# Layer 1's first keys and values, computed at the end of layer 0's attention

## The chip, the cores and the metric

The kernel runs on one core of a Trainium2 chip as one program. The metric is the device time of that program in microseconds (us). A core has five engines with a queue of instructions each: TensorE (PE in the profile) multiplies matrices from SBUF into PSUM, VectorE (DVE), ScalarE (ACT) and GpSimd (POOL) compute on SBUF and read PSUM, and SyncE (SP) here issues transfers. The engines wait for each other through semaphores. An instruction that waits holds up everything behind it in its own queue.

## The reference

Two layers follow each other on `x`, 16 sequences of 128 tokens with 256 features. Each layer is a cross-attention to a context `ctx` of the same shape, then a mixture of experts, both gated into the residual:

```python
x = x + tanh(g_xattn[0]) * attention0(layernorm(x), ctx, ctx)   # causal, 16 heads of 16
x = x + tanh(g_ffn[0])   * ffn0(layernorm(x))                   # top 2 of 16 experts + a shared expert
x = x + tanh(g_xattn[1]) * attention1(layernorm(x), ctx, ctx)   # rows of queries masked
x = x + tanh(g_ffn[1])   * ffn1(layernorm(x))                   # top 2 of 8 experts
```

Inside an attention, `q = layernorm(x) @ Wq + bq`, `k = ctx @ Wk + bk` and `v = ctx @ Wv + bv`, then softmax of the scaled products over the keys, times `v`, times `Wo`. What matters for this case: **the keys and values of layer 1 depend on the context and weights alone**, not on what layer 0 computes.

## The kernel before, in words

All of `x` stays in SBUF (`x_sb`, 16 batches side by side). Batches are handled in four groups of four. `attention(layer, ...)` returns the pieces of one layer's attention as functions:

- `load_kv(g)` (line 321) issues on SP the load of group g's context, 512 KB, into the tile `slot_cn`. In layer 1 every group uses the same half of this tile, so a load must wait until the products of the group before have read it.
- `keys(g, m)` (line 333) makes one of two halves of the group's keys: two matrix products (tile `psk`, line 337), and a ScalarE copy with bias into `slot_kq`. `vals(g, i)` (line 343) makes the values of two batches: four products (`psv`, line 348) and a ScalarE copy into `slot_v`. Two buffers each of keys, queries and values alternate by the parity of g.
- `constant()` (line 361) makes the product `bo` of the value bias with `Wo`.
- `q_stats`, `q_rows`, `q_turn`, `q_product` normalise a group's rows (GpSimd raises the variances to a power, tile `mvq`, lines 286 and 287; VectorE writes `xn_q`, line 296), transpose them (`nt_q`) and make the queries (`psq`, line 402).
- `run(...)` (line 599) is the loop over 32 units, a unit being half the heads of one batch. For each unit GpSimd spreads the keys (`kd`, line 429), TensorE makes the scores (`pss`, line 456), VectorE their maxima (`mx`, line 462), ScalarE the exponentials (`exps`, line 472), TensorE transposes them two units later (`pt`, line 484; copies `pT` by ScalarE and VectorE, lines 489 and 491) and multiplies with the values three units later (`pso`, line 505).

`run` has an order written out by hand for TensorE, VectorE and ScalarE (`tc.manual_schedule`). In each unit it calls, in order, the lists `first`, the scores, the transposes, the list `then`, the exponentials, the value products, and the lists `last` and `late`. The argument `fill` puts more calls into these lists. For the units after 34 they are appended to `then`. SP's and GpSimd's orders are left to the framework's planner, which places an instruction by when it expects its inputs.

At the end of layer 0's attention the dictionary `fill0` (line 946) puts in the shared expert: `shared_up(tb, c)` (products `pu`, line 921; Silu on ScalarE, line 927; product `hs` on VectorE, line 928) and `shared_down(tb, i)` (products `po`, line 934; added to `x_sb` on VectorE, line 940). In the same units the routing of the last group goes on: its rows (line 296), transposes (`nt_f`, line 308, called by `route_turn`), logits (`pr`, line 581), the long sequence of small VectorE steps in `send0` (lines 713 to 896), and GpSimd's scatters of the rows (line 852).

The tiles `psk`, `psv`, `po`, `pr`, `py`, `psq`, `pso`, `rank` and `bo` all come from one PSUM pool of two banks, `ps_o`. A product waits until the tile before it in its bank has been copied out.

Then come layer 0's routed experts, in 10 iterations of four tiles: SP fetches the rows (`xg`, line 1005, three buffers), TensorE transposes them (`xt`, line 1016), and the two products follow (lines 1038 and 1063). In this loop the results of group 0 are gathered back by GpSimd (`gather0`, tile `slot_y`, line 978) and added to `x_sb` on VectorE (`add0`, line 987), and group 0's queries for layer 1 are made. A branch that joins all engines follows (line 1119), then layer 1's `run`, with the remaining gathers and adds in its units. While it starts, SP loads 1 MB pieces of layer 1's expert weights (line 1344). The kernel ends with layer 1's experts, each of which adds its result to `xacc` by an indirect transfer (line 1479).

Layer 1's first products stand in two places. Group 0's `load_kv`, `keys`, `vals` and `constant` stand after layer 0's attention, before the first `xt`. Group 1's load is put into iteration 2 of the expert loop, and its `keys` and `vals` into units 0 to 3 of layer 1's `run`, by these lines:

```python
d = int(layer == 1 and g == 1)
if not d:
    put(first, u, load_kv, g)
for m in range(KD):
    put(then, u - d + 1 + m, keys, g, m)
for i in range(0, GB, 2):
    put(then, u - d + 3 + i // 2, vals, g, i)
```

Of the kernel before, what the change touches and what calls it, by code (L numbers as in the profile page):

```python
# [24 lines left out]
def kernel(ctx: ExitStack, tc: tile.TileContext, a: dict, out: bass.AP):  # L25
# [6 lines left out]
    NB, S, D = a["x"].shape  # L32
    assert S == P
    T = NB * S
    KD = D // P
# [4 lines left out]
    GB = 4  # L40
# [3 lines left out]
    E1, F1 = a["L1_ffn_W1"].shape[0], a["L1_ffn_W1"].shape[2]  # L44
# [70 lines left out]
    def load_attn(layer, eng, pool, at={}):  # L115
        pre = f"L{layer}_xattn_"
        w = {}
        for s in ("k", "q"):
            w["W" + s] = load_w(pre + "W" + s, D, eng, pool, at.get(s))
        for s in ("k", "q"):  # L120
            w["b" + s] = load_cols(pre + "b" + s, [P, KD], eng, pool)
        for s in ("v", "o"):
            w["W" + s] = load_w(pre + "W" + s, D, eng, pool, at.get(s))
        w["bv"] = pool.tile([P, KD], F32, name=f"c_{pre}bv", bufs=1)
        with nc.allow_non_contiguous_dma(reason="a column of 256"):
            eng.dma_start(w["bv"], a[pre + "bv"].rearrange("(k p) -> p k", p=P))
        w["bo"] = load_row(pre + "bo", D, eng, pool)
        return w
# [15 lines left out]
    attn_w = [load_attn(0, nc.scalar, ap0, weights_in("y")), {}]  # L144
# [169 lines left out]
    def attention(layer, E, w, dispatch):  # L314
# [109 lines left out]
        def spread(u):  # L424

            b, m = units[u]
            cols = slice((b % GB) * P, (b % GB + 1) * P)
            kd = ap.tile([P, HQ, P], F32, tag="kd", name=f"kd_{layer}_{u}", bufs=3)
            due["pool"] = nc.gpsimd.tensor_tensor(  # L429
                kd,  # L430
                groups[b // GB]["kT"][:, m, cols].unsqueeze(1).broadcast_to([P, HQ, P]),
                heads.unsqueeze(2).broadcast_to([P, HQ, P]),
                ALU.mult,
            )
            kds[u] = kd
# [158 lines left out]
        def route_send(g):  # L594

            rows, lg = routes.pop(g)
            return dispatch(g, lg, rows)

        def run(pool, along, fill, leave=False):


            nonlocal ap
            ap = pool
            NU = len(units)
            first, then, last, late = {}, {}, {}, {}
            senders = {}

            def piece(g):
                if g not in senders:
                    senders[g] = route_send(g)  # L610
                next(senders[g], None)

            def put(where, u, fn, *args):
                where.setdefault(u, []).append((fn, args))

            if layer == 0:
                for i in range(0, GB, 2):
                    put(then, i // 2, vals, 0, i)
                put(then, 2, constant)
            put(last, 3, add_constant, 0)  # L620
            for g in range(1, NG):
                u = (g - 1) * GB * KD

                d = int(layer == 1 and g == 1)
                if not d:
                    put(first, u, load_kv, g)
                for m in range(KD):
                    put(then, u - d + 1 + m, keys, g, m)
                for i in range(0, GB, 2):
                    put(then, u - d + 3 + i // 2, vals, g, i)  # L630
                for i in range(0, GB, 2):
                    put(last, u + d + i // 2, q_stats, g, i)
                    put(last, u + d + 1 + i // 2, q_rows, g, i)
                    put(then, u + d + 2 + i // 2, q_turn, g, i)
                for m in range(KD):
                    put(then, u + d + 5 + m, q_product, g, m)
                put(last, u + 7, add_constant, g)
            for b in range(NB):
                u = b * KD + KD - 1
                put(last, u + 2, inverse, b)  # L640
                put(then, u + 3, turn_inverse, b)
                put(last, u + 3, scale, b)
                put(then, u + 4, output, b)
                g = b // GB
                if b % 2 and not (leave and b == NB - 1):

                    d = int(b < NB - 1)
                    put(last if d else first, u + 5, route_rows, b - 1)
                    put(then, u + 5 + d, route_turn, b - 1, None)
                    put(late, u + 5 + d, route_product, b - 1)  # L650
                    if b % GB == GB - 1:
                        at = list(range(u + 7, u + 7 + MOST))
                        if g == NG - 2:

                            v = NB * KD + (3 if leave else 4)
                            at[SENDS:] = range(v, v + MOST - SENDS)
                            if leave:
                                at = [NB * KD + 1 + i // 2 for i in range(MOST)]
                        if g == NG - 1:
                            at = [u + 5 + (i + 1) // 3 for i in range(MOST)]  # L660
                        for i in at:
                            put(late, i, piece, g)
                put(first, b * KD, along, b)
            for u, fns in fill.items():
                fns = [(fn, args) for fn, *args in fns]
                if u < NU:
                    late[u] = fns + late.get(u, [])
                elif u < NU + 3:
                    then[u] = fns + then.get(u, [])
                else:  # L670
                    then[u] = then.get(u, []) + fns
            with tc.manual_schedule(engines=ENGINES):
                for u in range(2):

                    with tc.issue_after(due["pool"].ins):
                        spread(u)
                u = 0
                while u < NU or first or then or last or late:
                    for fn, args in first.pop(u, []):
                        fn(*args)  # L680
                    if u < NU:
                        if u + 2 < NU:
                            spread(u + 2)
                        scores(u)
                    if 0 <= u - 2 < NU:
                        turn(u - 2)
                    for fn, args in then.pop(u, []):
                        fn(*args)
                    if u < NU:
                        exps(u)  # L690
                    if 0 <= u - 3 < NU:
                        values(u - 3)
                    for fn, args in last.pop(u, []) + late.pop(u, []):
                        fn(*args)
                    u += 1
# [100 lines left out]
    def send0(g, sc, rows):  # L796
# [98 lines left out]
        nc.vector.tensor_reduce(sm, ex, AX.X, ALU.add)  # L895
        nc.vector.tensor_tensor(gate0[:, g, 1, :], sm, gate0[:, g, 0, :], ALU.mult)

    (load_kv, keys, _, _, q_stats, q_rows, q_turn, q_product, run), _ = attention(
        0, E0, attn_w[0], send0
    )  # L900
    load_kv(0)
# [28 lines left out]
    def shared_down(tb, i):  # L930
# [12 lines left out]
        )  # L943

    up, down = shared_up, shared_down
    fill0 = {
        32: [(up, 0, 0)], 33: [(up, 0, 1)], 34: [(up, 1, 0)], 35: [(down, 0, 0), (up, 1, 1)],
        36: [(down, 0, 2), (up, 2, 0)], 37: [(down, 1, 0), (up, 2, 1)],
        38: [(down, 1, 2), (up, 3, 0)], 39: [(down, 2, 0), (up, 3, 1)], 40: [(down, 2, 2)],
        41: [(down, 3, 0)], 42: [(down, 3, 2)],  # L950
    }
    run(ap0, lambda b: None, fill0)
    at0.close()
# [38 lines left out]
    with tc.tile_pool(name="f0", bufs=2, reuse_waits="tile") as fp:  # L992
# [10 lines left out]
        def fetch0(u):  # L1003
            xg = new0("xg", fp.tile, [P, UN, D], F32, tag="xg0", name=f"xg0_{u}", bufs=3)
            nc.sync.dma_start(
                xg, xs0[u * UN * P : (u + 1) * UN * P, :].rearrange("(j p) d -> p j d", p=P)
            )
            return xg
# [48 lines left out]
        def down0(u, hT):  # L1057
# [16 lines left out]
            )  # L1074

        NU = NH0
        dispatch1 = []
        got = [fetch0(0), fetch0(1)]
        (load_kv, keys, vals, constant, q_stats, q_rows, q_turn, q_product, run), route1 = (
            attention(1, E1, attn_w[1], lambda *z: dispatch1[0](*z))  # L1080
        )
        load_kv(0)
        for m in range(KD):
            keys(0, m)
        for i in range(0, GB, 2):
            vals(0, i)
        constant()


        extra, ahead = {}, {}  # L1090
        last = [-(-(2 * GT * (g + 1) + (E0 - 1) * P) // (UN * P)) for g in range(NG - 1)]
        assert last[0] + 4 == last[1] + 2 == last[2] == NU
        add = lambda where, u, fn, *args: where.setdefault(u, []).append((fn, args))
        u = last[0]
        add(extra, 2, load_kv, 1)
        for t in range(GB):
            add(extra, u, gather0, t)
        for i in range(0, GB, 2):
# [55 lines left out]
    ap1 = ctx.enter_context(tc.tile_pool(name="at1", bufs=2, reuse_waits="tile"))  # L1154
# [368 lines left out]
    def down_n(n):  # L1523
# [2 lines left out]
            out_rows if n >= len(order) - NL else xacc,  # L1526
        )

    run(ap1, beside, {
        **{KD * b + 1 + (b > 0): [(add0, t), (add0, t + 1)] for b, t in comes.items()},  # L1530
        31: [(get, 0), (get, 1)],
        33: [(turn_in, 0), (up_n, 0)],
# [8 lines left out]
    route_rows, route_turn, route_product, route_send = route1  # L1541
# [84 lines left out]
```

## Time and profile before

| | |
|---|---|
| median of 3 runs | 817.59 us (816.72 to 818.86) |
| the profiled execution's own time | 819.49 us |
| its span | 817.8 us |
| TensorE matrix products, busy | 739.6 us (90%) |
| VectorE, busy | 454.8 us (56%) |
| ScalarE, busy | 360.8 us (44%) |
| GpSimd, busy | 302.3 us (37%) |
| last `pu` of the shared expert starts | 238.43 us |
| first `psk` of layer 1 (group 0) starts | 251.43 us |
| first `xt` of the experts of layer 0 starts | 259.18 us |
| first `pss` of layer 1 starts | 337.91 us |

The span runs from the first to the last instruction of the profiled execution; times in the timelines count from its start. In a timeline, a row is a run of equal instructions: start, duration, engine, line, operation, the tile written and the tiles read, how many, and in brackets how long the engine was idle before and which instruction released it. The duration of pipelined matrix products overlaps the next row a little, so starts are better for counting than ends.

### The profile page before, as it was taken

The numbers are of one execution on the slowest core, as the hardware profiler recorded it, in microseconds if no ns is written. First come the engines' busy times: TensorE is split into PE (matmuls) and PEld (weight loads), VectorE is DVE, ScalarE is ACT, GpSimd is POOL, SyncE is SP. The second block draws the span as 40 slices with busy tenths as digits, with TensorE's granted clock in tenths as the row PEclk, the third lists the DMA queues.
The fourth block names the chain that finished last, engine by engine and source line by source line (L and its number), as shares of the span: only waits on it lengthen the run. The fifth ranks groups of instructions, "written<-read, shape, count | busy, mean of one in ns | idle before, by whom it ended". The sixth has DMA issues, their size and how long they took to land.

```text
span 817.8 us, 14876 instructions
## 1 busy us (share of the span) xinstructions
PE 739.6 (90%) x4960; PEld 550.0 (67%) x4960; DVE 454.8 (56%) x1214; ACT 360.8 (44%) x1431; POOL 302.3 (37%) x376
## 2 busy tenths in 40 slices
PE   7999989889898998879988987798999999999993
PEld 3556646555456886445645554687899999999982
DVE  4666698998483334588788779647222222222210
ACT  1677757675032332578767758221112222222220
POOL 6524226341222004763643524256323333223321
PEclk9999999999999999999999979899999999999997
DMA  8999992000015444781210402626766656666633
GB/s 283 377 346 200 343 331 75 14 34 21 26 38 168 138 147 129 257 283 48 70 41 14 156 20 72 239 67 195 241 184 187 196 166 174 190 194 187 178 57 116
DMA packets 88125, 126.80 MB, mean 155 GB/s; under 512 B 8544, under 2 KB 72832, under 8 KB 87888
## 3 DMA queue, kind: packets, MB, share of 16 engines
q1 hardware_dynamic: 75824, 106.41, 40.9%
q0 software_dynamic: 10144, 18.22, 8.8%
q10 hardware_dynamic: 2080, 1.19, 0.5%
q8 instruction: 43, 0.70, 0.4%
q14 instruction: 34, 0.28, 0.1%
HBM read 80.77 MB, written 47.13 MB: 156 GB/s over the span
## 4 chain that ended last, share of the span: by engine, by line
DMA 23%; PE 17%; DVE 10%; issue 3%; ACT 3%; POOL 1%; POOLq 0%; ACTq 0%; DVEq 0%; SPq 0%
DMA xacc<-y,xg 21%; PE pu L1448 4%; PE pss L456 2%; PE po L1469 2%; PE pt L484 2%; DVE mx L462 2%; ACT y L1478 2%; PE pso L505 1%; PE psq L402 1%; PE py L541 1%; DMA out_dram<-xacc 1%; PE psv L348 1%; DVE pT L491 1%; ACT hT L1459 1%; DVE st L283 1%
## 5 line engine op out<-in xcount | busy, mean ns | idle before, releaser
L472 ACT ACTIVATE p<-pss,mx 128x128 f32<-128x128 f32 x512 | 180.8, 390 | 10.2 <-DVE mx L462 10.0
L1448 PE MATMUL pu<-xT,w 128*128 128x128 f32 x1152 | 137.7, 279 | 5.9 <-DVE xT L1438 4.9
L1448 PEld LDWEIGHTS pu<-xT,w 128*128 128x128 f32 x1152 | 136.7, 195 | 9.4 <-DVE xT L1438 6.3
L472 ACT ACTIVATION_READ_ACCUMULATOR p<-pss,mx 128x1 f32 x512 | 117.3, 229 | 0.0
L1479 POOL DMA_INDIRECT xacc<-y,xg x34 | 54.4, 1600 | 146.7 <-ACT y L1478 118.1
L1469 PE MATMUL po<-w_sb,hT 128*128 x432 | 101.1, 384 | 0.6 <-issue 0.3
L429 POOL TENSOR_TENSOR kd<-slot_kq,heads 128x512 f32<-128x512 f32 x64 | 66.7, 1047 | 91.2 <-PE pss L456 88.5
L1478 ACT ACTIVATE y<-yb,gate 128x256 f32<-128x256 f32 x36 | 18.3, 508 | 184.6 <-DMA xacc<-y,xg 161.3
L1461 DVE TENSOR_SCALAR hT<-pu,bT_b 128x128 f32<-128x128 f32 x108 | 30.4, 344 | 123.6 <-ACT hT L1459 123.6
L484 PEld LDWEIGHTS pt<-ident,p 128*128 128x128 f32 x512 | 55.9, 143 | 49.9 <-issue 33.6
L1469 PEld LDWEIGHTS po<-w_sb,hT 128*128 128x128 f32 x432 | 80.4, 193 | 10.8 <-issue 0.6
L462 DVE TENSOR_REDUCE mx<-pss 128x8 f32<-128x1024 f32 x64 | 78.0, 1219 | 16.3 <-PE pss L456 16.2
L456 PE MATMUL pss<-kd,slot_kq 64*128 64x512 f32 x256 | 75.2, 665 | 1.7 <-POOL kd L429 1.2
L484 PE MATMUL pt<-ident,p 128*128 128x128 f32 x512 | 71.7, 283 | 0.9 <-ACT rT L527 0.5
L489 ACT COPY pT<-pt 128x512 f32<-128x512 f32 x64 | 39.4, 616 | 19.4 <-PE pt L484 19.3
L491 DVE COPY pT<-pt 128x512 f32<-128x512 f32 x64 | 43.6, 681 | 0.7 <-PE pt L484 0.7
L505 PE MATMUL pso<-pT,slot_v 128*32 128x128 f32 x1024 | 42.5, 285 | 0.0
L852 POOL DMA_INDIRECT xs<-rows,to x32 | 31.6, 987 | 28.1 <-DVE more L961 13.2
L1038 PE MATMUL pu0p<-w,xT 128*128 x160 | 38.4, 395 | 0.2 <-ACT xT L1021 0.2
L1459 ACT ACTIVATE hT<-pu,bT_b 128x128 f32<-128x128 f32 x108 | 30.8, 368 | 15.7 <-PE pu L1448 15.6
L1476 DVE TENSOR_TENSOR yb<-po,b_sb 128x256 f32<-128x256 f32 x36 | 15.3, 424 | 39.7 <-PE po L1469 39.1
L1225 POOL DMA_INDIRECT xs<-rows,toi x32 | 31.9, 997 | 14.5 <-issue 8.0
(277 smaller groups left out, 1190.3 us busy)
## 6 DMA issues: line engine op xcount, KB each, us to landing
w<-in_L_ffn_W_dram SPq DMA_DIRECT2D x36, 1024.0 KB, 5.2
xs<-zero SPq DMA_DIRECT2D x7, 2080.0 KB, 20.1
w<-in_L_ffn_W_dram SPq DMA_DIRECT2D x12, 512.0 KB, 8.3
xs<-zero SPq DMA_DIRECT2D x1, 6144.0 KB, 22.8
w_sb<-in_L_ffn_W_dram SPq DMA_DIRECT2D x6, 1024.0 KB, 12.9
xg<-xs SPq DMA_DIRECT2D x10, 512.0 KB, 3.8
yb<-y SPq DMA_DIRECT2D x10, 512.0 KB, 3.0
xg<-xs SPq DMA_DIRECT2D x39, 130.0 KB, 2.9
```

The source lines that it names most:

```text
L429: due["pool"] = nc.gpsimd.tensor_tensor(kd, groups[b // GB]["kT"][:, m, cols].unsqueeze(1).broadcast_to([P, HQ, P]), heads.unsqueeze(2).br ...
L456: nc.tensor.matmul(ps[:, j, :], qT[rows, m, cols], kd[rows].rearrange("p h k -> p (h k)"), start=(layer != 0), stop=True,)
L462: nc.vector.tensor_reduce(mx, s, AX.X, ALU.max, negate=True)
L472: nc.scalar.activation(p[:, h, :], s[:, h, :], AF.Exp, bias=mx[:, h : h + 1], accum_out=sums[b][:, m * HH + h : m * HH + h + 1],)
L484: nc.tensor.transpose(pt[:, i * P : (i + 1) * P], p[:, j * HQ + i, :], ident)
L489: nc.scalar.copy(pT, pt)
L491: nc.vector.tensor_copy(pT, pt)
L505: nc.tensor.matmul(o[r * VW : (r + 1) * VW, :], v[:, b % GB, m * HH + h, :], pT[h // HQ][:, (h % HQ) * P : (h % HQ + 1) * P], start=(x == ...
L1448: nc.tensor.matmul(ps[:, j, c * P : (c + 1) * P], wt[:, k, (j * 4 + c) * P : (j * 4 + c + 1) * P], xT[:, k * P : (k + 1) * P], start=(k == ...
L1459: nc.scalar.activation(dst, src, AF.Relu, bias=bias)
L1469: nc.tensor.matmul(po[:, :D], hT[:, c, :], w2_sb[c][:, bass.ds(e256, D)], start=(c == 0), stop=(c == FC1 - 1),)
L1479: nc.gpsimd.indirect_dma_start(out=dst, out_offset=bass.IndirectOffsetOnAxis(ap=xg[:, D : D + 1].bitcast(I32), axis=0), in_=y, in_offset=N ...
```

## The change

Layer 1's `attention(1, ...)` is set up before layer 0's `run` is called, and a function `kv(i)` is added to `fill0`. In the fill of layer 0's last units it issues group 0's load (unit 38), its keys (units 39 and 40, after the shared expert's products of that unit), its values (units 41 and 42, before them), and in unit 43 the whole of group 1: load, keys and values. The calls that did this later are taken out: group 0's before the first `xt`, group 1's load in the expert loop, and group 1's keys and values in layer 1's units 0 to 3. `constant()` stays where it was.

One more step is moved. The transposes of the last two batches' rows for the routing (`route_turn` of batch 14) leave the head of the list `then` of unit 36 and become `turn_last`, called after the first shared product of that unit.

```diff
-                for m in range(KD):
-                    put(then, u - d + 1 + m, keys, g, m)
-                for i in range(0, GB, 2):
-                    put(then, u - d + 3 + i // 2, vals, g, i)
+                for m in range(0 if d else KD):
+                    put(then, u + 1 + m, keys, g, m)
+                for i in range(0, 0 if d else GB, 2):
+                    put(then, u + 3 + i // 2, vals, g, i)
...
-                    put(then, u + 5 + d, route_turn, b - 1, None)
+                    if d:
+                        put(then, u + 6, route_turn, b - 1, None)
...
+    def kv(i):
+
+        if i == 0:
+            load_kv(0)
+        elif i < 3:
+            keys(0, i - 1)
+        elif i < 5:
+            vals(0, 2 * (i - 3))
+        else:
+            load_kv(1)
+            for m in range(KD):
+                keys(1, m)
+            for j in range(0, GB, 2):
+                vals(1, j)
+
+    def turn_last():
+        route0[1](NB - 2, None)
...
-        36: [(down, 0, 2), (up, 2, 0)], 37: [(down, 1, 0), (up, 2, 1)],
-        38: [(down, 1, 2), (up, 3, 0)], 39: [(down, 2, 0), (up, 3, 1)], 40: [(down, 2, 2)],
-        41: [(down, 3, 0)], 42: [(down, 3, 2)],
+        36: [(down, 0, 2), (turn_last,), (up, 2, 0)], 37: [(down, 1, 0), (up, 2, 1)],
+        38: [(down, 1, 2), (up, 3, 0), (kv, 0)], 39: [(down, 2, 0), (up, 3, 1), (kv, 1)],
+        40: [(down, 2, 2), (kv, 2)], 41: [(kv, 3), (down, 3, 0)], 42: [(kv, 4), (down, 3, 2)], 43: [(kv, 5)],
...
-        load_kv(0)
-        for m in range(KD):
-            keys(0, m)
-        for i in range(0, GB, 2):
-            vals(0, i)
         constant()
...
-        add(extra, 2, load_kv, 1)
...
-    run(ap1, beside, {
+    run1(ap1, beside, {
```

More of the change, by code (lines that the diff above doesn't have):

```diff
@@ L896, in send0 @@
         nc.vector.tensor_tensor(gate0[:, g, 1, :], sm, gate0[:, g, 0, :], ALU.mult)
-    (load_kv, keys, _, _, q_stats, q_rows, q_turn, q_product, run), _ = attention(
+    (load_kv, keys, _, _, q_stats, q_rows, q_turn, q_product, run), route0 = attention(
         0, E0, attn_w[0], send0
@@ L945 @@
     up, down = shared_up, shared_down
+    dispatch1 = []
+    (load_kv, keys, vals, constant, q_stats, q_rows, q_turn, q_product, run1), route1 = attention(
+        1, E1, attn_w[1], lambda *z: dispatch1[0](*z)
+    )
+    def kv(i):
[13 more added lines that the diff above has]
+        route0[1](NB - 2, None)
     fill0 = {
         32: [(up, 0, 0)], 33: [(up, 0, 1)], 34: [(up, 1, 0)], 35: [(down, 0, 0), (up, 1, 1)],
-        36: [(down, 0, 2), (up, 2, 0)], 37: [(down, 1, 0), (up, 2, 1)],
-        38: [(down, 1, 2), (up, 3, 0)], 39: [(down, 2, 0), (up, 3, 1)], 40: [(down, 2, 2)],
-        41: [(down, 3, 0)], 42: [(down, 3, 2)],
+        36: [(down, 0, 2), (turn_last,), (up, 2, 0)], 37: [(down, 1, 0), (up, 2, 1)],
+        38: [(down, 1, 2), (up, 3, 0), (kv, 0)], 39: [(down, 2, 0), (up, 3, 1), (kv, 1)],
+        40: [(down, 2, 2), (kv, 2)], 41: [(kv, 3), (down, 3, 0)], 42: [(kv, 4), (down, 3, 2)], 43: [(kv, 5)],
     }
@@ L1076 @@
         NU = NH0
-        dispatch1 = []
         got = [fetch0(0), fetch0(1)]
-        (load_kv, keys, vals, constant, q_stats, q_rows, q_turn, q_product, run), route1 = (
-            attention(1, E1, attn_w[1], lambda *z: dispatch1[0](*z))
-        )
-        load_kv(0)
-        for m in range(KD):
-            keys(0, m)
-        for i in range(0, GB, 2):
-            vals(0, i)
         constant()
```

## The prediction

> **What bounds the kernel now.** I read the page's chain first, then the chain in order of time, then each engine's timeline in two stretches: the end of layer 0's attention (216 to 260 us) and the first units of layer 1's attention (337 to 362 us). Those are the only places that the change touches.
>
> ```profile
> DMA xacc<-y,xg 21%; PE pu L1448 4%; PE pss L456 2%; PE po L1469 2%; PE pt L484 2%; DVE mx L462 2%; ACT y L1478 2%; PE pso L505 1%; PE psq L402 1%; PE py L541 1%; DMA out_dram<-xacc 1%; PE psv L348 1%; DVE pT L491 1%; ACT hT L1459 1%; DVE st L283 1%
> ```
>
> No single engine carries the end. From 580 us on it is one scatter-add after another, and before that it is the attention. All of it runs at fixed distances from what came before, so a microsecond gained or lost at 260 us arrives at the end unless something in between waits for something else. The timeline of TensorE (start, duration, work, idle before it and its releaser) at the end of layer 0's attention:
>
> ```profile
> 212.72 3.60 PE L921 MATMUL pu<-xnT,w_L_ffn_Ws 128*128 128x512 f32 x8
> 219.29 0.76 PE L308 MATMUL nt_f<-ident,rows 128*128 128x128 f32 x4 [2.97 <-DVE rows L296]
> 219.88 1.89 PE L934 MATMUL po<-w_L_ffn_Ws,hs 128*128 128x256 f32 x8
> 221.61 3.60 PE L921 MATMUL pu<-xnT,w_L_ffn_Ws 128*128 128x512 f32 x8
> ...
> 241.87 1.89 PE L934 MATMUL po<-w_L_ffn_Ws,hs 128*128 128x256 f32 x8
> 245.43 2.16 PE L934 MATMUL po<-w_L_ffn_Ws,hs 128*128 128x256 f32 x8 [1.67 <-DVE x_sb L940]
> 249.60 1.99 PE L934 MATMUL po<-w_L_ffn_Ws,hs 128*128 128x256 f32 x8 [2.02 <-DVE x_sb L940]
> 251.43 3.60 PE L337 MATMUL psk<-slot_cn,slot_w 128*128 128x512 f32 x8
> 254.87 3.62 PE L348 MATMUL psv<-slot_w,slot_cn 128*128 128x256 f32 x16
> 258.32 1.03 PE L368 MATMUL bo<-slot_w,c_L_xattn_bv 128*128 128x256 f32 x4
> 259.18 1.04 PE L1016 MATMUL xt<-ident,xg 128*128 128x128 f32 x8
> ```
>
> Here TensorE has three holes, all behind VectorE. Its last work before the experts (group 0's psk, psv, bo) is back to back, and xt, the experts' first transpose, follows with no hole. From there the expert loop is TensorE's: 39.13 us busy between 260 and 300 us. So **the start of xt is the number to work out**. The start-to-start distances are 1.72 for one of the two psk or psv halves (3.44 for a pair), 0.86 for bo, 1.73 for a po.
>
> Then the first units of layer 1, where group 1's products stand now (TensorE, then VectorE):
>
> ```profile
> 340.88 1.13 PE L456 MATMUL pss<-kd,slot_kq 64*128 64x512 f32 x4
> 341.94 1.99 PE L337 MATMUL psk<-slot_cn,slot_w 128*128 128x512 f32 x4
> 345.14 1.13 PE L456 MATMUL pss<-kd,slot_kq 64*128 64x512 f32 x4 [1.21 <-POOL kd L429]
> ...
> 361.45 0.69 PE L523 MATMUL rt<-ident,rs 128*128 128x128 f32 x2 [2.30 <-DVE pT L491]
> ```
> ```profile
> 348.78 0.49 DVE L987 SCALAR_TENSOR_TENSOR x_sb<-slot_y,gate,x_sb 128x256 f32<-128x256 f32 x1 [0.51 <-DMA slot_y<-yb,to]
> 349.18 1.22 DVE L462 TENSOR_REDUCE mx<-pss 128x8 f32<-128x1024 f32 x1
> ...
> 355.63 1.46 DVE L296 TENSOR_SCALAR xn_q<-x_sb,mvq 128x256 f32<-128x256 f32 x2 [1.19 <-POOL mvq L287]
> ```
>
> TensorE is *not* the bound here. It waits for GpSimd's kd, for the pT copies, and 2.30 us before rt. VectorE waits for the gathered rows (slot_y), runs on to 354.4, then waits for GpSimd's mvq. GpSimd is the slow one: eight gathers at about 1.27 us each.
>
> **Part 1, turn_last.** The transpose of the rows of batches 14 and 15 (nt_f) moves from before shared-expert product po(0,2) to after it. nt_f needs VectorE's rows (released at 219.29) and po does not. So po runs at 216.16 to 217.88, inside the old hole; nt_f still starts at 219.29 and the next pu at 219.88 instead of 221.61: **-1.73**. VectorE's following chain starts from ScalarE's Silu of that pu (VectorE idles 3.31 before 225.88), so it moves too: every time below is 1.73 earlier than its old counterpart.
>
> **Part 2, group 0's products between the shared expert's.** In the built kernel's order they stand as pu(3,1), psk, po(2,2), psk, psv, po(3,0), psv, po(3,2). They add no work, but they share two PSUM banks with the po tiles, so each start also waits for an eviction. pu(3,1) ends at 241.87 - 1.73 = 240.14.
> - psk: 240.14 to 241.86. ScalarE evicts it behind the last Silu (old 243.40, now 241.67 to 242.27), 0.69 long: 242.96.
> - po(2,2) takes that bank: 243.05 to 244.77, a hole of 1.19.
> - second psk: its bank is free at 245.37 - 1.73 = 243.64; runs 244.77 to 246.49. Eviction 1.92 after its start (251.43 to 253.35 in the trace), 0.69 long: 247.38. ScalarE's exponential zex before it, which waits for VectorE, ends at 245.85 and does not hold it.
> - psv: same bank, 247.45 to 249.17, a hole of 0.96. po(3,0): 249.17 to 250.89 (VectorE's eviction of po(2,2) ends at 249.5 - 1.73 = 247.8). Second psv 250.89 to 252.61, po(3,2) 252.61 to 254.33.
>
> **Part 3, group 1's load and products before xt.** Group 1's context overwrites the tile (slot_cn) that group 0's last psv reads, so SP's load waits for 252.61 plus about 0.2. Queued behind it on SP are the first three fetches of expert rows (xg), free from 253.67 - 1.73 = 251.95; they start about 1.3 later, land by 257 (median 3.8), and xt needs the first only at 263.9, so this is hidden with 6.9 to spare. Landing of the load, from the tile's view:
>
> ```profile
> DMA to landing us min/median/max: 3.3/7.1/15.0
> ```
>
> I take the low end, 3.3: it is the row of the load at 258.51, in a stretch where the DMA engines are 12 to 42% busy; 7.1 and more belong to stretches that are full. So psk of group 1 starts at 252.8 + 3.3 = 256.15, a hole of 1.8; two psk and two psv end at 256.15 + 4 x 1.72 = 263.03 (evictions on two banks keep up), bo 0.86, **xt at 263.89 against 259.18: +4.7**. Counted another way: +6.9 of products, and the holes, measured start to start, go from about 7.4 to 5.4. With the load at 7.1 it is +8.5; with the three new holes (3.97) gone it is +0.7.
>
> A second SP effect: group 2's load is also hoisted, to behind the third xg fetch (its tile is free when group 1's psv ends). The fetch behind it waits for the first xt anyway: 0.
>
> **Part 4, what layer 1's start gives back.** Removed there: 4 x 1.72 = 6.9 of TensorE, two 0.7 and two 0.6 evictions of ScalarE. The full 6.9 would come back only if TensorE were the bound. Following the waits without these products: the second pss could start at 338.97, so mx(1) comes 0.4 earlier; but the next adds wait for gathers issued at 339.28 to 344.0, after the branch that joins the engines, and the last lands at 348.78. mx(2) stays at 349.18, exps(2) at 350.44, mx(3) at 352.64, then the mvq wait. Give-back: **0** (ends 0 and -2, the latter if the gathers land faster; nearer 0 since no gather moves).
>
> GpSimd's order changes by one step: a kd (1.03) now goes ahead of the mvq pair that VectorE waits for at 355.63. mvq is 1.03 later, but the xn_q that took 1.05 beside the old kd (its twin took 0.40) then runs alone: **+0.2** (ends 0 and +1).
>
> *A rule against the change.* The removal leaves TensorE idle from 340.03 to 345.14. The windows view (start:end, length, busy PE, PEld, DVE, ACT, POOL, granted clock, DMA share, GB/s) after the existing 2.30 us hole:
>
> ```profile
> 359.00:362.00 3.00, 0.70 (x4) 0.29 (x2) 2.39 (x3) 0.59 (x1) 1.56 (x2) 0.87 1.09 369
> 362.00:365.00 3.00, 3.00 (x22) 1.20 (x22) 1.68 (x4) 2.83 (x16) 0.62 (x1) 0.56 0.28 102
> ```
>
> The clock falls to 0.56 and the pso and pss there take 1.08 and 1.90 instead of 0.65 and 1.13: 1.2 lost. The Trainium skill, "TensorE: Matmul & The Clock Gate", Part 1, halves the clock only after an idle window of about 3.4 us; by it, the 2.3 hole should have been harmless and the new one of 5.1 is not. By either the next pss and pt run cold and lose about 1.7 together. I count 0: pss would end at 347.0 and pt at 348.9, and mx(2) starts at 349.18 and the copies of pt after it. With that cover gone the sum is +1.2 more, as in the row. The holes before xt are no longer than the old ones of 2.97 and 2.02, after which the clock stayed at 1.00 in the windows from 195 to 260 us.
>
> **Sum.** -1.73 and the rest of the stretch make +4.7, layer 1 gives 0, GpSimd +0.2: **+4.9**. The profiled execution took 819.49 (span 817.80, 1.69 around it); its sum is span 822.7. It stands 1.9 above the median of the runs shown, 817.59, so the median predicted is 817.6 + 4.9 = **822.5**.
>
> **Rivals.**
> - *Layer 1 gives the products back (not slower).* If TensorE sets units 0 to 3, 6.9 returns: 817.6 + 4.9 - 6.9 = 815.6. For it: pss at 340.88 stands right behind psk, and TensorE is 90% busy over the span. Against it: the 1.21 and 2.30 us waits and the slot_y wait above. It decides once the give-back passes 4.9 - 2.5 = 2.4.
> - *The new holes do not form.* The load or the evictions come sooner and xt is +0.7: 818.5. Against: the load's tile is read until 252.6, and no landing of it is below 3.3.
> - *The load is slow, or the new idle leaves TensorE cold on the path.* +3.8 or +1.2: 823.7 to 826.3. For: 7.1 median. Against: a mostly idle DMA.
> - *turn_last does not do what it says* (VectorE does not follow): +1.73, 824.2.
>
> **How the numbers follow.** Main case (two to three holes, no give-back, 821 to 824): 0.66; slower cases 0.16; holes partly absent or a give-back of some 2 (818.5 to 820.5) 0.10; full give-back 0.08. A measurement of this kernel tells about 0.3% (2.5 us) from no change: 815.1 and 820.0 are the limits. Slower 0.83, same 0.12, faster 0.05. Range 819.0 to 825.2: it leaves out the full give-back and the slow load.
>
> **What would show it.** Right: a hole-free po(0,2) before nt_f; xt 4 to 5.5 us later than 259.2; psk of group 1 released by the DMA of slot_cn, its start about 3.5 after the end of group 0's last psv; rt of unit 4 still waiting for pT, its distance from the first pss of layer 1 (337.91 to 361.45, 23.5) unchanged within 1. Wrong: that distance shorter by 2.5 or more; xt within 2 of 259; or the distance from xt to the end changed elsewhere.

## The result, and the profile after

The changed kernel is slower: 825.66 us median against 818.62 us for the kernel before in the same comparison, **ratio 1.0085, 95% interval 1.0063 to 1.0106** (10 runs each). That is about +7.0 us, where +4.9 was forecast, and the median lies 0.5 us above the stated range. Of the distance to the forecast 822.5, 1.0 us is not the change's: the range was built on three runs of the kernel before (817.59), and in these ten it is 818.62. The profiled execution has a span of 827.6 us; it was the slowest of the ten, so its distances are used below more than its span.

TensorE's timeline at the end of layer 0's attention, kernel after (start, duration, work, idle before it and its releaser):

```profile
212.65 3.60 PE L922 MATMUL pu<-xnT,w_L_ffn_Ws 128*128 128x512 f32 x8
216.08 1.89 PE L935 MATMUL po<-w_L_ffn_Ws,hs 128*128 128x256 f32 x8
219.21 0.76 PE L308 MATMUL nt_f<-ident,rows 128*128 128x128 f32 x4 [1.24 <-DVE rows L296]
219.81 3.60 PE L922 MATMUL pu<-xnT,w_L_ffn_Ws 128*128 128x512 f32 x8
...
236.63 3.60 PE L922 MATMUL pu<-xnT,w_L_ffn_Ws 128*128 128x512 f32 x8
240.07 1.88 PE L337 MATMUL psk<-slot_cn,slot_w 128*128 128x512 f32 x4
242.84 1.99 PE L935 MATMUL po<-w_L_ffn_Ws,hs 128*128 128x256 f32 x8 [0.89 <-ACT slot_kq L341]
244.67 1.88 PE L337 MATMUL psk<-slot_cn,slot_w 128*128 128x512 f32 x4
247.32 1.99 PE L348 MATMUL psv<-slot_w,slot_cn 128*128 128x256 f32 x8 [0.78 <-issue]
249.16 1.89 PE L935 MATMUL po<-w_L_ffn_Ws,hs 128*128 128x256 f32 x8
250.88 1.89 PE L348 MATMUL psv<-slot_w,slot_cn 128*128 128x256 f32 x8
252.61 1.99 PE L935 MATMUL po<-w_L_ffn_Ws,hs 128*128 128x256 f32 x8
257.59 5.37 PE L337 MATMUL psk<-slot_cn,slot_w 128*128 128x512 f32 x8 [2.98 <-DMA slot_cn<-in_ctxT_dram]
262.79 3.62 PE L348 MATMUL psv<-slot_w,slot_cn 128*128 128x256 f32 x16
266.25 1.03 PE L368 MATMUL bo<-slot_w,c_L_xattn_bv 128*128 128x256 f32 x4
267.11 1.04 PE L1041 MATMUL xt<-ident,xg 128*128 128x128 f32 x8
```

Up to 252.61 every start is within 0.25 us of the forecast. Then group 1's psk waits 2.98 us for its load, and the psk pair takes 5.20 from start to start instead of 3.44. xt starts at 267.11 instead of the forecast 263.89 (259.18 before). The same hole and what follows it in the windows view (start:end, length, busy PE, PEld, DVE, ACT, POOL, granted clock, DMA share, GB/s):

```profile
254.00:257.60 3.60, 0.62 (x4) 0.23 (x2) 0.75 (x1) 0.00 (x0) 0.00 (x0) 1.00 0.86 242
257.60:261.20 3.60, 3.60 (x6) 1.65 (x7) 0.00 (x0) 0.69 (x1) 0.00 (x0) 0.67 1.00 333
```

While TensorE waits, the DMA engines are 86% busy. While psk runs, the granted clock is 0.67.

The first units of layer 1 in the kernel after:

```profile
346.98 1.13 PE L456 MATMUL pss<-kd,slot_kq 64*128 64x512 f32 x4 [0.18 <-DVEq L1134]
353.93 2.08 PE L456 MATMUL pss<-kd,slot_kq 64*128 64x512 f32 x4 [5.82 <-POOL kd L429]
355.94 1.97 PE L484 MATMUL pt<-ident,p 128*128 128x128 f32 x8
...
369.63 0.69 PE L523 MATMUL rt<-ident,rs 128*128 128x128 f32 x2 [2.46 <-DVE pT L491]
```

VectorE's maxima of that third pss come after an add that waits for gathered rows:

```profile
356.79 0.48 DVE L1012 SCALAR_TENSOR_TENSOR x_sb<-slot_y,gate,x_sb 128x256 f32<-128x256 f32 x1 [0.74 <-DMA slot_y<-yb,to]
357.20 1.22 DVE L462 TENSOR_REDUCE mx<-pss 128x8 f32<-128x1024 f32 x1
```

Where group 1's four products stood, TensorE now idles 5.82 us, and the next pss and pt take 2.08 and 1.97 instead of 1.13 and 1.09. rt still waits for pT. From the first pss (345.67) to rt it takes 23.96, against 23.54 before: nothing came back.

So of the kernel's stages, counted from the last pu of the shared expert to cancel what differs earlier between executions:

| distance, us | before | after |
|---|---|---|
| start of the pu behind nt_f to the last pu | 16.82 | 16.82 |
| last pu to xt | 20.75 | 30.48 |
| xt to first pss of layer 1 | 78.73 | 78.56 |
| first pss to rt | 23.54 | 23.96 |

Up to rt, all of the loss is in one row. It is +9.7 there, and the 1.73 gained at nt_f, ahead of these rows, is the counterweight (from the pu before nt_f to the last pu it takes 23.98 instead of 25.71). From rt to the end of the span it takes 456.35 before and 457.97 after, but 453.85 in a second profile of the changed kernel (further down): what single executions differ by there says nothing of the change.

### The profile page after: what moved, and what is told of

Read it like the earlier page. It is cut to its first block, busy times and chain, and to the rows that moved or that the text cites. A ratio compares the mean times of both kernels' runs of the same rounds, so it can differ in the third digit from the quotient of the medians.

```text
span 827.6 us, 14874 instructions
## 1 busy us (share of the span) xinstructions
PE 744.8 (90%) x4960; PEld 554.3 (67%) x4960; DVE 455.0 (55%) x1214; ACT 362.4 (44%) x1431; POOL 302.3 (37%) x376
## 3 DMA queue, kind: packets, MB, share of 16 engines
q10 hardware_dynamic: 2080, 1.19, 0.5%
## 4 chain that ended last, share of the span: by engine, by line
PE 39%; DVE 9%; DMA 3%; issue 3%; ACT 2%; POOL 1%; another core or an unknown queue 1%; POOLq 0%; DVEq 0%; ACTq 0%; SPq 0%
PE pu L1463 15%; PE po L1484 13%; PE pt L484 2%; PE pss L456 2%; DVE mx L462 2%; PE pso L505 2%; PE psq L402 1%; DMA out_dram<-xacc 1%; PE py L541 1%; DMA xacc<-y,xg 1%; PE xt L1451 1%; PE pr L581 1%; DVE pT L491 1%; ACT p L472 1%
## 5 line engine op out<-in xcount | busy, mean ns | idle before, releaser
L1463 PE MATMUL pu<-xT,w 128*128 128x128 f32 x1152 | 139.6, 281 | 6.3 <-DVE xT L1453 3.1
L1463 PEld LDWEIGHTS pu<-xT,w 128*128 128x128 f32 x1152 | 138.6, 197 | 10.0 <-DVE xT L1453 4.4
L484 PEld LDWEIGHTS pt<-ident,p 128*128 128x128 f32 x512 | 57.7, 146 | 50.1 <-issue 33.7
L484 PE MATMUL pt<-ident,p 128*128 128x128 f32 x512 | 73.8, 289 | 0.6 <-ACT rT L527 0.5
```

The lines of the kernel that those rows point to most:

```text
L484: nc.tensor.transpose(pt[:, i * P : (i + 1) * P], p[:, j * HQ + i, :], ident)
L1463: nc.tensor.matmul(ps[:, j, c * P : (c + 1) * P], wt[:, k, (j * 4 + c) * P : (j * 4 + c + 1) * P], xT[:, k * P : (k + 1) * P], start=(k == ...
```

## The experiments

The theory after this reading: the loss is group 1's products on TensorE's path (6.9), plus a load that lands later than forecast, plus a low clock that the hole leaves. The rivals: interleaving group 0 costs something; the products' removal from layer 1 does give something back, and the loss is elsewhere; the load is no part of it. Each comparison has its own runs of the kernel before beside it; single executions of one kernel spread by about 1%, so the ratios decide on totals and the profiles on stages.

### Group 0's part alone

```diff
-                for m in range(0 if d else KD):
-                    put(then, u + 1 + m, keys, g, m)
-                for i in range(0, 0 if d else GB, 2):
-                    put(then, u + 3 + i // 2, vals, g, i)
+                for m in range(KD):
+                    put(then, u - d + 1 + m, keys, g, m)
+                for i in range(0, GB, 2):
+                    put(then, u - d + 3 + i // 2, vals, g, i)
...
-        40: [(down, 2, 2), (kv, 2)], 41: [(kv, 3), (down, 3, 0)], 42: [(kv, 4), (down, 3, 2)], 43: [(kv, 5)],
+        40: [(down, 2, 2), (kv, 2)], 41: [(kv, 3), (down, 3, 0)], 42: [(kv, 4), (down, 3, 2)],
...
+        add(extra, 2, load_kv, 1)
```

> Group 0's products between the shared expert's and the moved transposes, as in the changed kernel, but group 1's load, keys and values where they were before. My theory (the whole loss is group 1's work put on the path, with its load): xt starts near 255.2 instead of 259.2, so about 4.0 us faster than before, 0.995. The rival that interleaving itself costs (shared PSUM banks, evictions queued behind ScalarE's Silu and Exp): no faster than before, and holes of more than 2 us between pu and the last po.

Measured: ratio 1.0017 (0.9998 to 1.0036). Neither theory as written. The end of its TensorE timeline before the experts:

```profile
251.85 1.89 PE L935 MATMUL po<-w_L_ffn_Ws,hs 128*128 128x256 f32 x8
253.58 1.03 PE L368 MATMUL bo<-slot_w,c_L_xattn_bv 128*128 128x256 f32 x4
258.32 1.97 PE L1041 MATMUL xt<-ident,xg 128*128 128x128 f32 x8 [3.71 <-DMA xg<-xs]
260.11 5.96 PE L1063 MATMUL pu0p<-w,xT 128*128 x16
```

Interleaving did its work: bo starts 17.7 us after the last pu (235.88), where before it started 19.9 after. But then xt waits 3.71 for the expert rows, and xt and the first pu0p run slow (5.96 against 3.98). Group 1's load had been planned ahead of the row fetches on SP again; it waits there for group 0's last psv, and the rows land 5.7 to 7.6 us after their issue instead of 3.8 to 4.9. Whether the rows could come sooner is left to the last run.

### The moved transposes alone

```diff
-                    put(then, u + 5 + d, route_turn, b - 1, None)
+                    if d or layer:
+                        put(then, u + 5 + d, route_turn, b - 1, None)
...
-        36: [(down, 0, 2), (up, 2, 0)], 37: [(down, 1, 0), (up, 2, 1)],
+        36: [(down, 0, 2), (turn_last,), (up, 2, 0)], 37: [(down, 1, 0), (up, 2, 1)],
```

> The kernel before with the last rows' transposes moved behind po(0,2), nothing else. My theory: the next pu starts 1.7 earlier and all that follows with it, 1.7 us faster, 0.998. The rival, that VectorE's small steps do not follow: no difference, and the hole turns up again before a later po.

Measured: ratio 0.9990 (0.9965 to 1.0014). The total alone does not tell 1.7 us from nothing. In its profile the last pu starts 23.98 us after the pu before nt_f (212.09 to 236.07), where it took 25.71 before (212.72 to 238.43), and xt follows 20.74 later (20.75 before): the 1.73 is there, VectorE did follow, and no hole turned up again.

### A tile of its own for group 1's context

```diff
-            if layer == 0 and g % 2:
+            if (layer == 0 and g % 2) or (layer == 1 and g == 1):
...
         if i == 0:
             load_kv(0)
+            load_kv(1)
...
-            load_kv(1)
             for m in range(KD):
                 keys(1, m)
```

> The changed kernel, with group 1's context loaded early into a tile of its own, so that its first psk has no load to wait for. My theory now (the hole before psk of 2.98 and the low clock after it are the excess over the forecast): no hole and a psk pair of 3.44 instead of 5.2, xt near 262.1, about 3 us slower than before (1.004) and 4 to 5 faster than the changed kernel. The rival, that the excess comes from layer 1's start or from the end: as slow as the changed kernel, 1.0085.

Measured: ratio 1.0019 (0.9995 to 1.0043). The expected 1.004 lies just inside the interval, and the whole interval lies under the changed kernel's. The psk pair follows the last po with no hole:

```profile
253.47 1.89 PE L935 MATMUL po<-w_L_ffn_Ws,hs 128*128 128x256 f32 x8
255.20 3.60 PE L337 MATMUL psk<-cT,slot_w 128*128 128x512 f32 x8
```

From the last pu to xt it is 25.45, 5.0 less than in the changed kernel: 3.25 for the hole (start to start) and 1.76 for the clock. Against before it is 4.70 more, less the 1.73 at nt_f, plus 1.06 between xt and the first pss in this execution: some 4 slower by the stages, while the interval reaches only to 3.5. Where the rest went is not shown: from rt to the end, single executions of the kernels here that leave nothing out take 450.3 to 458.0.

In this run the load of group 2, of the same size, stands on SP where group 1's load stands in the changed kernel, but with one row fetch right behind it instead of three. It landed in 4.1:

```profile
DMA to landing us min/median/max: 4.1/4.1/4.1
```

### Layer 1's first units without the products

```diff
-                for m in range(KD):
-                    put(then, u - d + 1 + m, keys, g, m)
-                for i in range(0, GB, 2):
-                    put(then, u - d + 3 + i // 2, vals, g, i)
+                for m in range(0 if d else KD):
+                    put(then, u - d + 1 + m, keys, g, m)
+                for i in range(0, 0 if d else GB, 2):
+                    put(then, u - d + 3 + i // 2, vals, g, i)
```

> The kernel before with group 1's keys and values of layer 1 left out altogether (their tiles hold what layer 0 left there). My theory, that TensorE is not the bound in layer 1's first units: 0 to 0.5 us from before, 1.000. The rival, that the products set the time there: 6.9 us faster, 0.992.

Measured: ratio 1.0144 (1.0118 to 1.0170), which fits neither. The total cannot be read: the attention results are wrong, and layer 1's experts compute more products than before, probably because rows are routed differently. The count of products pu, here and in the kernel before:

```profile
L1448 PE MATMUL pu<-xT,w x1184: 272/275/550, 513.6 to 804.5; 128*128 128x128 f32 x198
```
```profile
L1448 PE MATMUL pu<-xT,w x1152: 272/275/582, 516.3 to 796.5; 128*128 128x128 f32 x192
```

The stage in question lies before that and can be read: from the first pss (338.73) to rt (362.56) it takes 23.83, against 23.54 before. Taking 6.9 us of TensorE's work out of it saves nothing.

This profile shows one thing more. Up to layer 1 it is the kernel before, and TensorE has the same hole of 2.97 before nt_f. In the profile of the kernel before, the clock stayed at 1.00 behind it. Here po takes 3.09 behind it instead of 1.89:

```profile
218.71 1.11 PE L308 MATMUL nt_f<-ident,rows 128*128 128x128 f32 x4 [2.97 <-DVE rows L296]
219.61 3.09 PE L934 MATMUL po<-w_L_ffn_Ws,hs 128*128 128x256 f32 x8
222.54 3.60 PE L921 MATMUL pu<-xnT,w_L_ffn_Ws 128*128 128x512 f32 x8
```

The granted clock from 219.0 to 222.5 us is 0.57 here and 1.00 there, and the next pu starts 3.83 after nt_f instead of 2.32. So behind the same hole, in the same part of the program, the clock can be high in one execution and low in another.

### The products a second time

To the changed kernel, group 1's keys and values were added again in units 0 to 3, with the lines of `run` as they were before. With this the load of group 2 and GpSimd's order of kd and mvq go back to their old places too.

> The changed kernel with group 1's keys and values computed a second time in layer 1's units 0 to 3, where they were before (the same values into the same tiles). My theory, that TensorE is not the bound there: the same time as the changed kernel within 0.5, from the first pss to rt 23.5 to 24. The rival, that the removal gives 6.9 back there: up to 6.9 slower than the changed kernel, 1.017.

Measured: ratio 1.0072 (1.0050 to 1.0094), and the changed kernel beside it, on the same chip:

> The changed kernel once more, beside the three others. Both theories: 0.7 to 1.0 per cent slower than before (1.0085 was measured), with psk of group 1 released by its load after a hole of about 3 us, and 5.2 us for the pair.

Measured: ratio 1.0077 (1.0048 to 1.0106), its hole 2.97, its psk pair 5.21. So 6.9 us more of TensorE's work in layer 1's first units costs nothing that can be measured: the medians are 823.44 with it and 825.06 without, with intervals that overlap, and nowhere the +6.9 of the rival. First pss to rt is 23.54 with the products and 23.85 without. **TensorE is not the bound there**, shown from both sides: by taking the products out and by adding them.

### TensorE kept busy in the hole

```diff
             load_kv(1)
+            busy = psum_t("busy")
+            for _ in range(3):
+                nc.tensor.matmul(busy, ident, xnT[:, 0, :GT], start=True, stop=True)
             for m in range(KD):
                 keys(1, m)
```

> The changed kernel with three products without use (0.86 each) on TensorE in the hole before group 1's psk. My theory that the low clock after the hole is a cost of its own: psk still waits for the load to the same time, but the pair takes 3.44 instead of 5.2, xt 1.8 sooner, 1.5 to 2 us faster than the changed kernel, 1.0065. The rival that psk is slow for another reason (the load's traffic): still 5.2, no gain or a small loss.

```profile
252.38 1.99 PE L935 MATMUL po<-w_L_ffn_Ws,hs 128*128 128x256 f32 x8
254.22 2.74 PE L964 MATMUL busy<-xnT,ident 128*128 128x512 f32 x6
257.29 3.67 PE L337 MATMUL psk<-slot_cn,slot_w 128*128 128x512 f32 x8 [0.34 <-DMA slot_cn<-in_ctxT_dram]
260.80 3.62 PE L348 MATMUL psv<-slot_w,slot_cn 128*128 128x256 f32 x16
```

psk is released by the load at nearly the same time (257.29 against 257.37 in the changed kernel's second run), and the pair now takes 3.51: the low clock is a cost of its own, 1.7 us, and goes with the hole and not with the load's traffic, which is the same. That rests on this one profile, against three with the hole open, which all have the slow pair (5.20, 5.21 and 5.20). xt is 1.8 sooner (265.11 against 266.90). The total does not show the gain: 1.0078 (1.0056 to 1.0099), where 1.0065 was expected. Half is lost again by the first pss (344.90 against 345.80), since the pu0p behind the later hole before nt_q took 5.29 here and 4.74 there; the rest is below what the interval can tell.

### The load without the fetches beside it

```diff
             for m in range(KD):
                 keys(1, m)
+                if m == 0:
+                    nc.tensor.matmul(
+                        psum_t("hold")[:, :8], due["sg"][:, :P], due["sg"][:, :8],
+                        start=True, stop=True,
+                    )
```

`due["sg"]` is the last Silu tile; the first fetch of expert rows overwrites its buffer and so waits for this product.

> The changed kernel, with a tiny product (128x8, without use) behind the first half of group 1's keys that reads a buffer which the first expert fetch overwrites, so that the three expert fetches on SP wait for it and group 1's load has the DMA engines to itself. My theory (the load took 4.7 and not 3.3 because the three fetches behind it share the engines, and the hole of 3 that this makes is what lowers the clock): landing in 3.3 to 3.6, a hole of 1.5 to 1.9, psk at full clock (3.44 for the pair), xt about 27.5 after the last pu instead of 30.7, 3 us faster than the changed kernel, 1.004. The rival that the load takes 4.7 by itself there: hole and low clock as in the changed kernel, 1.0077.

```profile
252.13 1.89 PE L936 MATMUL po<-w_L_ffn_Ws,hs 128*128 128x256 f32 x8
255.84 1.96 PE L337 MATMUL psk<-slot_cn,slot_w 128*128 128x512 f32 x4 [1.82 <-DMA slot_cn<-in_ctxT_dram]
257.63 0.28 PE L966 MATMUL hold<-sgs 128*128 128x8 f32 x2
257.77 1.96 PE L337 MATMUL psk<-slot_cn,slot_w 128*128 128x512 f32 x4
...
263.89 1.04 PE L1047 MATMUL xt<-ident,xg 128*128 128x128 f32 x8
```

Measured: ratio 1.0038 (1.0014 to 1.0062). The load lands 3.4 us after its issue; the hole is 1.82 and the clock stays at 1.00 (254 to 260 us). xt starts 27.73 after the last pu, as expected, 2.98 less than the changed kernel's 30.71 in its second run. The landing in the changed kernel itself is not in its profile, but from the load's issue to its first psk it takes 4.66 to 5.02 in the four profiles with three fetches behind it, and 3.52 here. In the run of group 0's part alone, where the load also had three fetches behind it, the landing was recorded. From the tile's view, first this run, then that one:

```profile
DMA to landing us min/median/max: 3.4/3.4/3.4
```
```profile
DMA to landing us min/median/max: 4.7/4.7/4.7
```

This is close to the forecast's own case. Its hole counts 1.98 from start to start where 1.82 was forecast, and xt comes 27.73 after the last pu where the forecast has 27.19. That xt starts at 263.89 in both is chance, since this execution's last pu is 0.5 earlier. At 1.0038 it is about 3.1 us slower than before (1.1 to 5.1), and the forecast's 4.9 lies inside.

### A version that keeps the gain

Group 0's part and the moved transposes, group 1 as before, and its load ordered behind the first fetches of expert rows. The lines in which it differs from the run of group 0's part alone:

```diff
-            nc.sync.dma_start(
+            due["fetch"] = nc.sync.dma_start(
...
+        def load_late():
+            with tc.issue_after(due["fetch"].ins):
+                load_kv(1)
+
-        add(extra, 2, load_kv, 1)
+        add(extra, 2, load_late)
```

> Group 0's products between the shared expert's and the moved transposes, group 1 as before, and its load put behind the first expert fetches on SP. My theory (in the run without this the fetches of expert rows stood behind that load, landed late, left a hole of 3.7 and a low clock): xt waits at most 2 us for the rows, stays at full clock, and starts 2 to 3.5 sooner than before: 2.5 us faster than before, 0.997. The rival, that the rows come no sooner because the scatters set them: the hole of 3.7 and the low clock stay, 1.001.

```profile
253.59 1.99 PE L935 MATMUL po<-w_L_ffn_Ws,hs 128*128 128x256 f32 x8
255.42 1.03 PE L368 MATMUL bo<-slot_w,c_L_xattn_bv 128*128 128x256 f32 x4
256.71 1.09 PE L1041 MATMUL xt<-ident,xg 128*128 128x128 f32 x8 [0.27 <-DMA xg<-xs]
258.05 3.98 PE L1063 MATMUL pu0p<-w,xT 128*128 x16 [0.24 <-ACT xT L1046]
```

Measured: **ratio 0.9955 (0.9935 to 0.9976)**, 814.50 against 817.75: faster than both kernels. xt waits 0.27 for the rows and starts at 256.71, 2.5 us sooner than before and 19.4 after the last pu. The first fetch is issued 15.5 after the last pu, where behind the load it was 16.7, and xt starts 3.9 after it instead of 5.7. So the hole of 3.71 and the low clock behind it are gone: the fetches neither wait behind the load nor share the engines with it.

## Why the prediction was right and wrong

- **Direction and mechanism: right.** Group 1's products were put on TensorE's path before xt and returned nothing in layer 1.
- **turn_last, -1.73: right.** po fills the hole before nt_f, the next pu starts at 219.81 (forecast 219.88), and from there to the last pu it takes 16.82 as before.
- **Group 0's products: right.** Holes of 1.19 and 0.96 were forecast (start to start); they are 1.05 and 0.93. The last po starts at 252.61, as forecast.
- **The load: wrong, and this is the step that failed.** The forecast put the landing at 3.3 us and named the three fetches behind it on SP only as things that wait. Part 3 asked whether the fetches would be late, and xt did not wait for them; it did not ask what they do to the load. SP's queue in the kernel after:

```profile
252.80 0.38 SPq L325 DMA_DIRECT2D slot_cn<-in_ctxT_dram  x1
253.36 1.46 SPq L1030 DMA_DIRECT2D xg<-xs  x3
```

  The fetches start 0.56 us after the load and share its engines: psk starts 4.79 after the load's issue, and the hole is 3.25 from start to start instead of 1.82, **+1.4**. With the load alone it is 1.98. The reading that gave 3.3 was wrong too. The 12 to 42% are means over stretches of 25 and 19 us. While that load moved, in the kernel before, the DMA engines were 89% busy (the share is the last figure but one):

```profile
258.50:261.80 3.30, 3.06 (x17) 2.14 (x17) 1.47 (x3) 2.46 (x3) 0.00 (x0) 1.00 0.89 293
```

  So 3.3 was no landing on idle engines. It was also the value of one execution: the same load in the same place took 4.0 in the run of the moved transposes alone and 4.1 in the run that left the products out.
- **The clock before xt: wrong, a term put at 0.** The forecast counted 0 because the hole was to be 1.8, and older holes of 2.97 and 2.02 had left the clock at 1.00. The real hole of 2.98 did not: psk took 5.20 instead of 3.44, **+1.76**. The hole of 1.82 in the run with the load alone left the clock at 1.00, so by that one profile the term follows from the load. The comparison with the older hole rested on one execution; in the run that left the products out, that very hole of 2.97 was followed by a clock of 0.57. And the prediction's own row had the clock fall to 0.56 behind a hole of 2.30. By the Trainium skill, "TensorE: Matmul & The Clock Gate", Part 1, the clock falls after an idle window of about 3.4 us, and 2.98 would have been harmless; the measurement decides. With these two terms the forecast sum is 4.9 + 1.4 + 1.8 = 8.1, inside the interval of the result (5.2 to 8.7). (The second count in part 3 gives 6.9 - 2.0 = 4.9 for xt and not 4.7; the miss does not hang on that.)
- **Give-back 0: right,** from both sides. GpSimd's changed order was put at +0.2; first pss to rt became 0.4 longer, and 0.3 in the second run of the changed kernel and in the run that left the products out.
- **The cold pss after the hole of 5 us in layer 1: right.** The hole is 5.82, pss and pt take 2.08 and 1.97, and mx still waits for the gathered rows.
- **The rivals.** The one that came true is the third, a slow load or a cold TensorE on the path (823.7 to 826.3, with 0.16). Its sizes were not right: the load cost 1.4 more and not 3.8, the low clock 1.76 and not 1.2. They stood there as alternatives. In all three profiles with the hole of 2.76 to 2.98 they came together, so they should have been added and given more weight. The range ended at 825.2, inside that rival instead of past it.

## What to carry to other kernels

Price a transfer with what will be issued right behind it, not with the mean traffic of a longer stretch of the kernel before: here three fetches behind a load made it land in 4.7 us instead of 3.4. Work that is moved off a stage saves only if its engine sets that stage; look for what ends the engine's waits there before counting a gain. A load that waits for a buffer holds up everything behind it in its queue, so it belongs behind the transfers that are ready: that order alone made xt's wait for the rows 0.27 us instead of 3.71. And one execution in which a hole left the clock high is no proof that the next one will.

## What the runs showed of the hardware

- A 512 KB load landed in 3.4 us alone, in 4.1 with one transfer of 512 KB issued 0.56 us after it on the same queue, and in 4.7 with three, each read in one profile. With three fetches ahead of it and one issued 1.7 us behind it, the same load took 3.3, 4.0 and 4.1 in three profiles.
- TensorE's clock fell after a hole of 2.76 to 2.98 us before psk in three of three profiles (5.20 or 5.21 for a psk pair; 3.51 in the one where the hole was filled with useless products) and stayed at 1.00 after one of 1.82.
- The hole of 2.97 before nt_f left the clock at 1.00 in the profile of the kernel before and was followed by 0.57 in that of the run that left the products out, with the same program up to there. So in this range neither the length of a hole nor the program around it decides alone; what does is open.
